# Gated cross-attention with routed experts: two of seven products added from PSUM, routing cut finer on two engines, another order of fetches, first expert block and biases

## The chip, the cores and the metric

The kernel runs on one core of one Trainium2 chip. The core has five engines with a queue of instructions each, worked off in order: TensorE (PE; its weight loads, PEld, run beside its matmuls), VectorE (DVE), ScalarE (ACT), GpSimd (POOL) and SyncE (SP, which issues DMAs here). [...]GpSimd has no part in reading PSUM here: what a matmul leaves is taken out by VectorE or ScalarE. The metric is the time of one execution on the device in microseconds, lower is better; the time of a version is the median of its runs.

## The reference

The input x is 32 sequences of 112 tokens of width 256, each with a context of 375 rows of width 256. All numbers are fp32.

```python
# cross-attention: latents = layernorm(x), context normalized too
lat = layer_norm(_layernorm(x)); ctx = layer_norm(context)
q = lat @ Wq                                   # 16 heads of 64
k, v = split(concat([ctx, lat], axis=1) @ Wkv) # 487 keys per sequence
attn = softmax(q @ k.T * 64**-0.5)
x = x + tanh(g_xattn) * ((attn @ v) @ Wout)

# experts: 8, two per token, 3584 tokens
xf = _layernorm(x)
scores = softmax(xf @ gate_w); topk_scores, topk_idx = top_k(scores, 2)
topk_scores /= sum(topk_scores)
h = gelu(xf @ w1[e] + b1[e]); y = h @ w2[e] + b2[e]
x = x + tanh(g_ffn) * sum over the two experts of (topk_score * y)
```

The expert layer is 256 to 1024 to 256 wide. A token's result needs only its two experts.

## The kernel before

**Attention loop.** The 16 heads are 8 pairs, and two sequences form a group g (16 groups). The main loop has 128 iterations n; n % 8 is the place m in the group. Each iteration attends with two head pairs of one sequence: `scores(n + 1)` (L451) makes the next iteration's scores, `nmx` (L461, VectorE) their negative maxima, `exps` (L471, ScalarE) the exponentials with their sums, `norm` (L483 `rc` on VectorE, L485 on ScalarE) divides by the sums, `turn_attn` (L492) transposes the weights four times per iteration (h = 0 to 3) into PSUM, and L496 copies each transpose to `exT` on VectorE. Every second iteration `attend` (L506) multiplies by the values, and L521 copies the result out on ScalarE.

**Sevens.** Keys and values of two sequences come from a 2x2 block product, which is done with seven products instead of eight (Strassen's way in Winograd's form): `input_sums` (L333, GpSimd, four subtractions in each group's m = 4) prepares the inputs, `seven` does the products. Each iteration does one seven's worth of products, half of a key seven and half of a value seven. Of the seven, 1, 6, 7 and 5 are copied from PSUM by ScalarE (L400, L404, L409, L414) and then added to each other on GpSimd (L394); products 2, 4 and 3 are added from PSUM by VectorE (L420). Within an iteration they stand in this order: last product and product 1, transposes h = 0; query unit (L310, L317), another last one, h = 1; product 6 and the third last one, h = 2; product 7, h = 3; product 5.

**Buffers.** All of these results, and the transposes, take their turns in the four PSUM buffers of the pool `ps_m`; the scores have two of their own. A matmul that gets a buffer waits until the instruction that empties it has run, so the place of that instruction on its engine decides when TensorE goes on.

**Order.** The order on every engine is the order in which the program is written (`tc.manual_schedule`): between the units of an iteration stand lists of filler, `pe[h]`, `dve[h]`, `soon_`, `outgoing` and `extra`, of which one part runs after each transpose h. In the filler are the layer norms of later inputs (m = 0, 2, 6, 7), the turning of inputs (m = 1, 3), and for each finished slab of 128 tokens the output projection (L541), the residual (L551), `normed` (L569, then a copy on GpSimd, L572) and the gate logits (`logits_of`, L579: eight per slab, two after each transpose, in m = 2 and 3 for one slab and m = 4 and 5 for the other).

**Routing.** Slabs are routed in groups of four (two at the end). `route_parts` gives 11 parts: largest logit, its first place, the rest, the same again for the second, then counts, places (two matmuls on PE, L665 and L668), gates and slots. One part runs after each transpose, on VectorE but for one tanh. Afterwards each token row is scattered to its place in `xg` by indirect DMAs of GpSimd (L699, eight per group, one after each transpose). The first group also finds row numbers for padded places (`strangers`, L724, L736).

**Experts.** From n = 122 (`LAST - 6`) the tail is prepared: six blocks of 128 rows are fetched (`fetch_rows`, L887, SP), then the weights of block 0 (`fetch_weights`, L900, SP). `hidden` (L918, gelu at L925 on ScalarE) and `second` (L931) do a block; blocks 0 and 1 run within n = 126 and 127. `biased` (L941) adds b2, `combine` (L947, L948) multiplies by the gate and adds the rows to the output with an indirect DMA of GpSimd. After the loop the last two slabs are projected, normalized and routed, while TensorE does blocks 0 to 2. A block's weights are fetched only if its expert isn't the one that lies there.

## Time and profile before

| | |
|---|---|
| median of 3 runs | 2190.36 us (2190.22 to 2191.26) |
| profiled execution | 2192.12 us |
| its span, first to last instruction | 2190.4 us |
| mean granted TensorE clock | 0.995 |
| scores, L451, 1024 matmuls | 242.0 us, 591 ns each |
| transposes, L492, 2048 matmuls | 283.6 us, 261 ns each |
| hidden, L918, 1920 matmuls | 229.3 us, 278 ns each |
| GpSimd additions of sevens, L394 | 1214 to 1332 ns each by form |
| DMA | 138.19 MB, mean 63 GB/s |

Busy times of engines overlap, and a matmul's duration is longer than its distance to the next, since matmuls are pipelined. A row of the timeline has start, duration, engine, line, operation, output and inputs, shapes and count; in brackets stands how long the engine had been idle before and what ended that. A row may merge several instructions that follow each other. Lines are those of the kernel before.

### The profile page before, as it was taken

What the parts mean: (1) busy time and instruction counts of PE and PEld (TensorE: products, weight loads), DVE (VectorE), ACT (ScalarE), POOL (GpSimd) and SP (SyncE); (2) the same over time, 40 slices, a digit from 0 to 9 for tenths busy, and PEclk for the clock granted to TensorE, in tenths of its full rate; (3) what the DMA queues carried; (4) which work ended last, traced back from release to release, by engine and by line L of the source; (5) the groups of instructions that cost most, each with busy time, mean ns of one, the idle gap of its engine ahead of it and who ended that gap; (6) DMA issues with size and microseconds to landing.
All of it is one profiled execution on the core that took longest, in us unless ns stands there. A gap on an engine that the chain in (4) does not pass through costs nothing. (4 is left out here: it accounts for less than half of the span.)

```text
span 2190.4 us, 41776 instructions
## 1 busy us (share of the span) xinstructions
PE 2137.0 (98%) x15944; PEld 1663.3 (76%) x15944; DVE 1251.8 (57%) x2758; ACT 1271.5 (58%) x3017; POOL 1005.3 (46%) x1136
## 2 busy tenths in 40 slices
PE   9999999999999999999999999999999899999998
PEld 5777777677777777777776777677777789999998
DVE  5567676867676767665767676756676531111111
ACT  5666666556766666667665666566665433434433
POOL 6645454455556545554546454555445222222222
PEclk9999999999999999999999999999999999999999
DMA  6692000010001000100000000000002346656553
GB/s 146 201 328 66 17 13 18 13 34 13 15 13 37 13 17 13 46 1 15 13 19 28 20 13 26 18 18 4 10 4 81 100 108 186 192 157 162 136 141 67
DMA packets 113699, 138.19 MB, mean 63 GB/s; under 512 B 14704, under 2 KB 101432, under 8 KB 113368
## 3 DMA queue, kind: packets, MB, share of 16 engines
q1 hardware_dynamic: 101032, 119.11, 17.7%
q0 software_dynamic: 11328, 15.33, 4.0%
q8 instruction: 127, 2.08, 0.4%
q10 hardware_dynamic: 1136, 1.05, 0.2%
q14 instruction: 76, 0.62, 0.1%
HBM read 166.84 MB, written 48.99 MB: 99 GB/s over the span
## 5 line engine op out<-in xcount | busy, mean ns | idle before, releaser
L485 ACT ACTIVATE ex<-ex,rc 112x487 f32<-112x487 f32 x512 | 331.1, 694 | 331.6 <-DVE rc L483 331.1
L461 DVE TENSOR_REDUCE nmx<-ps_s 112x2 f32<-112x974 f32 x256 | 287.5, 1164 | 336.8 <-PE ps_s L451 336.5
L471 ACT ACTIVATE ex<-ps_s,nmx 112x487 f32<-112x487 f32 x512 | 337.6, 668 | 152.7 <-DVE nmx L461 151.1
L496 DVE COPY exT<-ps_t 122x448 f32<-122x448 f32 x512 | 316.0, 617 | 105.7 <-PE ps_t L492 105.3
L492 PEld LDWEIGHTS ps_t<-ident,ex 112*122 112x122 f32 x2048 | 233.0, 139 | 131.4 <-issue 77.5
L925 ACT ACTIVATE h<-ps_h,b 128x128 f32<-128x128 f32 x480 | 175.5, 367 | 262.0 <-PE ps_h L918 222.0
L492 PE MATMUL ps_t<-ident,ex 112*122 112x112 f32 x2048 | 283.6, 261 | 10.1 <-ACT qT L317 3.5
L451 PE MATMUL ps_s<-kT,qT 64*112 64x487 f32 x1024 | 242.0, 591 | 0.0
L948 POOL DMA_INDIRECT out_dram<-y,xs x60 | 93.2, 1553 | 318.6 <-DVE y L947 200.1
L918 PE MATMUL ps_h<-xsT,w 128*128 128x128 f32 x1920 | 229.3, 278 | 7.5 <-issue 6.6
L918 PEld LDWEIGHTS ps_h<-xsT,w 128*128 128x128 f32 x1920 | 227.0, 194 | 12.5 <-issue 8.3
L506 PEld LDWEIGHTS ps_o<-exT,vv 122*64 122x64 f32 (+1 forms) x4096 | 197.6, 136 | 45.6 <-ACT kT L409 31.5
L931 PE MATMUL ps_y<-w,h 128*128 128x256 f32 x960 | 216.8, 379 | 0.0
L394 POOL TENSOR_TENSOR tmpv<-vv,tmpv 122x512 f32<-122x512 f32 x64 | 81.3, 1270 | 287.0 <-ACT tmpv L404 287.0
L506 PE MATMUL ps_o<-exT,vv 122*64 122x112 f32 (+1 forms) x4096 | 211.4, 260 | 0.8 <-DVE vv L420 0.8
L394 POOL TENSOR_TENSOR vv<-tmpv,vv 122x512 f32<-122x512 f32 x128 | 166.2, 1299 | 92.9 <-ACT vv L414 60.6
L384 PE MATMUL ps_v<-wkv_s,tT 128*122 128x128 f32 x1536 | 203.0, 275 | 0.2 <-POOL wkv_s L323 0.2
L378 PE MATMUL ps_k<-tT,wkv_s 128*128 128x487 f32 x378 | 191.7, 590 | 5.6 <-ACT tmpk L404 3.2
L931 PEld LDWEIGHTS ps_y<-w,h 128*128 128x128 f32 x960 | 178.0, 190 | 21.8
L384 PEld LDWEIGHTS ps_v<-wkv_s,tT 128*122 128x122 f32 x1536 | 183.1, 186 | 3.0 <-issue 1.3
L384 PEld LDWEIGHTS ps_v<-wkv,kvT 128*122 128x122 f32 x1024 | 125.8, 185 | 76.1 <-issue 53.1
L394 POOL TENSOR_TENSOR kT<-tmpk,kT 128x487 f32<-128x487 f32 x126 | 154.0, 1225 | 46.5 <-ACT kT L414 38.9
(203 smaller groups left out, 3307.1 us busy)
## 6 DMA issues: line engine op xcount, KB each, us to landing
w<-in_L_ffn_w_dram SPq DMA_DIRECT2D x120, 1024.0 KB
xg<-pad SPq DMA_DIRECT2D x8, 3640.0 KB
cin<-in_ctx_dram SPq DMA_DIRECT2D x32, 336.0 KB
xs<-xg SPq DMA_DIRECT2D x60, 130.0 KB
b<-in_L_ffn_b_dram SPq DMA_DIRECT2D x60, 128.0 KB
xin<-in_x_dram SPq DMA_DIRECT2D x32, 112.0 KB
x<-in_x_dram SPq DMA_DIRECT2D x28, 128.0 KB
out_dram<-x SPq DMA_DIRECT2D x28, 128.0 KB
```

The costliest lines, as they stand in the source:

```text
L378: nc.tensor.matmul(ps, lhsT=w[:, 0, i * P : (i + 1) * P], rhs=x[:, :NK], start=True, stop=True)
L384: nc.tensor.matmul(ps[:, c, :], lhsT=x[:, c * KC : (c + 1) * KC], rhs=w[:, 1, i * P : (i + 1) * P], start=True, stop=True,)
L394: nc.gpsimd.tensor_tensor(v[o], v[l], v[r], ALU.add)
L451: nc.tensor.matmul(ps[:, j, :NK], lhsT=qT[b // 2, i][r, b % 2, :], rhs=kT[b, i][r, :], start=True, stop=True,)
L461: nc.vector.tensor_reduce(nmx[b, i], pss[b, i][:, :, :NK], AX.X, ALU.max, negate=True)
L471: nc.scalar.activation(t[:, j, :NK], ps[:, j, :NK], AF.Exp, bias=nmx[b, i][:, j : j + 1], accum_out=sm[b, i][:, j : j + 1],)
L485: nc.scalar.mul(ex[b, i][:, j, :NK], ex[b, i][:, j, :NK], rc[:, j : j + 1])
L492: nc.tensor.transpose(ps[:, c, :], ex[b, i][:, j, c * KC : (c + 1) * KC], ident[:S, :S])
L496: nc.vector.tensor_copy(exT[b, i, j], ps)
L506: nc.tensor.matmul(ps[y * DH : (y + 1) * DH, r, x * S : (x + 1) * S], lhsT=vv[j][:m, c, x, r, y * DH : (y + 1) * DH], rhs=exT[2 * g + x, i ...
L918: nc.tensor.matmul(ps, lhsT=w1t[:, k, f * P : (f + 1) * P], rhs=xsT[t][:, k, :], start=(k == 0), stop=(k == KD - 1),)
L931: nc.tensor.matmul(psy[t], lhsT=hid[t][:, f, :], rhs=w2t[:, f, :], start=(f == 0), stop=(f == NF - 1),)
```

## The change

`exT` at h = 2 is copied by ScalarE. Products 6 and 7 are added from PSUM by VectorE. In an iteration `norm` stands directly behind the transpose's copy, ahead of the filler. Routing has 13 parts in place of 11; those that need no reduction and no PSUM go to the engine that is handed in, GpSimd in the loop and VectorE for the last group, and the first part runs two transposes earlier. The six row fetches come an iteration later, behind the weights of block 0. Block 0's first hidden unit moves from h = 0 of n = 126 to h = 1, behind both exps. `y` has three buffers of its own (two before, the pool's), and the biases of blocks 1 and 2 are added before the weight fetches that reuse their buffers.

```diff
             def p6():
                 new("t", None)
-                nc.scalar.copy(v["t"], product(6, s2, t2))
-                add("t", "11", "t")
+                nc.vector.tensor_tensor(v["t"], product(6, s2, t2), v["11"], ALU.add)
 
             def p7():
                 new("21", (a, i + NG))
-                nc.scalar.copy(v["21"], product(7, s3, t3))
-                add("21", "t", "21")
+                nc.vector.tensor_tensor(v["21"], product(7, s3, t3), v["t"], ALU.add)
...
-            nc.vector.tensor_copy(exT[b, i, j], ps)
+            (nc.scalar.copy if h == 2 else nc.vector.tensor_copy)(exT[b, i, j], ps)
...
-        def route_parts(g):
+        def route_parts(g, eng):
...
+            def equal(n, src):
+                at = new(f"s{n}", [P, RG, E])
+                nc.vector.tensor_tensor(at, src, over_e(v[f"m{n}"]), ALU.is_equal)
+                eng.tensor_tensor(at, at, over_b(rank, RG), ALU.mult)
...
             def rest():
-                first()
-                nc.vector.scalar_tensor_tensor(
-                    v["rest"], v["s1"], -BIG, logits, ALU.mult, ALU.add
-                )
+                nc.vector.tensor_tensor(v["s1"], v["s1"], over_e(v["top1"]), ALU.is_equal)
+                eng.tensor_scalar(new("rest", [P, RG, E]), v["s1"], -BIG, None, ALU.mult)
+                eng.tensor_tensor(v["rest"], v["rest"], logits, ALU.add)
 
             def apart():
-                second()
...
+                nc.vector.tensor_tensor(v["s2"], v["s2"], over_e(v["top2"]), ALU.is_equal)
...
+                eng.tensor_tensor(new("th", [P, RG]), v["m1"], v["m2"], ALU.subtract)
+                eng.tensor_tensor(new("both", [P, RG, E]), v["s1"], v["s2"], ALU.add)
+
+            def counts():
+
+                both, had = v["both"], new("had", [P, RG, E])
+                eng.tensor_copy(had[:, 0, :], macc)
+                for j in range(1, RG):
+                    eng.tensor_tensor(had[:, j, :], had[:, j - 1, :], both[:, j - 1, :], ALU.add)
+                eng.tensor_tensor(macc, had[:, RG - 1, :], both[:, RG - 1, :], ALU.add)
...
             def slots_of():
+                for s in (v["s1"], v["s2"]):
+                    eng.tensor_tensor(s, s, v["place"], ALU.mult)
...
-            ys[t] = found["tiles"].tile([P, D], F32, tag="y", name=f"y_{t}")
+            ys[t] = found["tiles"].tile([P, D], F32, tag="y", name=f"y_{t}", bufs=3)
...
-                        r, (hits, ids, ids_out) = route_parts(group[i][0])
-                        extra = [[], []] + [[part] for part in r[:10]]
+                        r, (hits, ids, ids_out) = route_parts(group[i][0], nc.gpsimd)
+                        extra = [[part] for part in r[:11]]
...
                 found["early"] = ctx.enter_context(tc.tile_pool(name="early", bufs=1, side="right"))
+                fetch_weights(0)
+            if n == LAST - 5:
                 for t in range(NE):
                     fetch_rows(t)
-                fetch_weights(0)
...
-                pe[0] += [lambda: others(ends), lambda: hidden(0, 0, 1)]
-                pe[1] += [lambda: hidden(0, 1, 3)]
+                pe[0].append(lambda: others(ends))
+                pe[1] += [lambda: hidden(0, 0, 3)]
...
                 turn_attn(n, h)
+                if more and h in (1, 3):
+                    norm(n + 1, h // 2)
                 then_ = soon_[:]
...
                     exps(n + 1, 1)
-                if more and h in (1, 3):
-                    norm(n + 1, h // 2)
...
-        r, _ = route_parts(g)
-        do(r[:7])
+        r, _ = route_parts(g, nc.vector)
+        do(r[:8])
         second(1)
+        biased(1)
         fetch_weights(4)
-        r[7]()
+        r[8]()
         second(2)
+        biased(2)
         fetch_weights(5)
```

More of the change, by code (lines that the diff above doesn't have):

```diff
@@ L594, in over_b @@
             return v.unsqueeze(1).to_broadcast([P, n, E])
-        def first_largest(src, n, g, found):
-            mx = rt.tile([P, src.shape[1]], F32, tag=f"mx{n}", name=f"mx{n}_{g}")
-            at = rt.tile([P, src.shape[1], E], F32, tag=f"sel{n}", name=f"sel{n}_{g}")
-            top = rt.tile([P, src.shape[1]], F32, tag=f"top{n}", name=f"top{n}_{g}")
-            found[f"m{n}"], found[f"s{n}"] = mx, at
-            def largest():
-                nc.vector.tensor_reduce(mx, src, AX.X, ALU.max)
-                nc.vector.tensor_tensor(at, src, over_e(mx), ALU.is_equal)
-            def where_first():
-                nc.vector.tensor_tensor(at, at, over_b(rank, src.shape[1]), ALU.mult)
-                nc.vector.tensor_reduce(top, at, AX.X, ALU.max)
-            def first():
-                nc.vector.tensor_tensor(at, at, over_e(top), ALU.is_equal)
-            return [largest, where_first, first]
-        def route_parts(g):
+        def route_parts(g, eng):
             RG, b0 = groups[g], begin[g]
@@ L626, in new, with largest @@
                 return v[tag]
-            choice = first_largest(logits, 1, g, v)
-            new("rest", [P, RG, E])
-            choice += first_largest(v["rest"], 2, g, v)
-            first, second = choice[2], choice[5]
+            def largest(n, src):
+                nc.vector.tensor_reduce(new(f"m{n}", [P, RG]), src, AX.X, ALU.max)
+            def equal(n, src):
+                at = new(f"s{n}", [P, RG, E])
+                nc.vector.tensor_tensor(at, src, over_e(v[f"m{n}"]), ALU.is_equal)
+                eng.tensor_tensor(at, at, over_b(rank, RG), ALU.mult)
@@ L633, in rest, with first @@
+            def first(n):
+                nc.vector.tensor_reduce(new(f"top{n}", [P, RG]), v[f"s{n}"], AX.X, ALU.max)
             def rest():
-                first()
-                nc.vector.scalar_tensor_tensor(
-                    v["rest"], v["s1"], -BIG, logits, ALU.mult, ALU.add
-                )
+                nc.vector.tensor_tensor(v["s1"], v["s1"], over_e(v["top1"]), ALU.is_equal)
+                eng.tensor_scalar(new("rest", [P, RG, E]), v["s1"], -BIG, None, ALU.mult)
+                eng.tensor_tensor(v["rest"], v["rest"], logits, ALU.add)
@@ L639, in apart @@
             def apart():
-                second()
-                th = new("th", [P, RG])
-                nc.vector.tensor_tensor(th, v["m1"], v["m2"], ALU.subtract)
-            choice[2], choice[5] = rest, apart
-            def both():
-                nc.scalar.activation(v["th"], v["th"], AF.Tanh, scale=0.5)
-                nc.vector.tensor_tensor(new("both", [P, RG, E]), v["s1"], v["s2"], ALU.add)
-                nc.vector.tensor_copy(new("had", [P, RG, E])[:, 0, :], macc)
-            def counts():
-                both, had = v["both"], v["had"]
-                for j in range(1, RG):
-                    nc.vector.tensor_tensor(
-                        had[:, j, :], had[:, j - 1, :], both[:, j - 1, :], ALU.add
-                    )
-                nc.vector.tensor_tensor(macc, had[:, RG - 1, :], both[:, RG - 1, :], ALU.add)
@@ L662, in places @@
-            def places():
+                nc.vector.tensor_tensor(v["s2"], v["s2"], over_e(v["top2"]), ALU.is_equal)
[7 more added lines that the diff above has]
+                eng.tensor_tensor(macc, had[:, RG - 1, :], both[:, RG - 1, :], ALU.add)
@@ L663, in places @@
+            def places():
+                nc.scalar.activation(v["th"], v["th"], AF.Tanh, scale=0.5)
                 ps = ps_m.tile([P, RG, E], F32, tag="m", name=f"ps_pos_{g}")
                 v["ps"] = ps
-                nc.tensor.matmul(
-                    ps, lhsT=before, rhs=v["both"], start=True, stop=False
-                )
+                nc.tensor.matmul(ps, lhsT=before, rhs=v["both"], start=True, stop=False)
                 nc.tensor.matmul(ps, lhsT=ones, rhs=v["had"], start=False, stop=True)
@@ L675, in gates @@
                 half = new("half", [P, RG])
-                nc.vector.tensor_scalar(half, v["th"], tg[:, 2:3], None, ALU.mult)
-                nc.vector.tensor_scalar(xr[g][:, :, 0, D], half, tg[:, 2:3], None, ALU.add)
-                nc.vector.tensor_scalar(
+                eng.tensor_scalar(half, v["th"], tg[:, 2:3], None, ALU.mult)
+                eng.tensor_scalar(xr[g][:, :, 0, D], half, tg[:, 2:3], None, ALU.add)
+                eng.tensor_scalar(
                     xr[g][:, :, 1, D], half, -1.0, tg[:, 2:3], ALU.mult, ALU.add
@@ L681, in gates, with out_to @@
                 for k in range(2):
-                    soon_.append(
-                        lambda k=k: nc.gpsimd.tensor_copy(
-                            xr[g][:, :, k, D + 1].bitcast(I32), tok[:, b0 : b0 + RG]
-                        )
+                    nc.gpsimd.tensor_copy(
+                        xr[g][:, :, k, D + 1].bitcast(I32), tok[:, b0 : b0 + RG]
                     )
             def slots_of():
-                place = v["place"]
+                for s in (v["s1"], v["s2"]):
+                    eng.tensor_tensor(s, s, v["place"], ALU.mult)
+            def out_to():
                 slot = new("slot", [P, 2, RG])
                 for k, s in enumerate((v["s1"], v["s2"])):
-                    nc.vector.tensor_tensor(s, s, place, ALU.mult)
                     nc.vector.tensor_reduce(slot[:, k, :], s, AX.X, ALU.add)
@@ L755, in strangers_out @@
                 )
-            parts = choice + [both, counts, places, gates, slots_of]
+            parts = [
+                lambda: largest(1, logits),
+                lambda: equal(1, logits),
+                lambda: first(1),
+                rest,
+                lambda: largest(2, v["rest"]),
+                lambda: equal(2, v["rest"]),
+                lambda: first(2),
+                apart,
+                counts,
+                places,
+                gates,
+                slots_of,
+                out_to,
+            ]
             return parts, (stranger_hits, stranger_ids, strangers_out)
@@ L1175 @@
                             extra.append([ids_out])
-                        extra.append(r[10:])
+                        extra += [[part] for part in r[11:]]
             if n == LAST - 8:
@@ L1258 @@
         turn_rows(3, nc.scalar.copy)
-        r, _ = route_parts(g)
-        do(r[:7])
+        r, _ = route_parts(g, nc.vector)
+        do(r[:8])
         second(1)
+        biased(1)
         fetch_weights(4)
-        r[7]()
+        r[8]()
         second(2)
+        biased(2)
         fetch_weights(5)
-        r[8]()
+        r[9]()
         found["ps"] = counted()
-        r[9]()
-        now()
-        r[10]()
+        do(r[10:])
         do(outgoing)
```

## The prediction

> **What bounds the kernel now.** I read the page's busy times first.

> ```profile
> PE 2137.0 (98%) x15944; PEld 1663.3 (76%) x15944; DVE 1251.8 (57%) x2758; ACT 1271.5 (58%) x3017; POOL 1005.3 (46%) x1136
> ```

> TensorE is busy all the time, and the change leaves its matmuls as they are. So the other engines matter only where TensorE waits for them, mostly for one of the four buffers of ps_m. To find these waits I cut the main loop into its iterations. A stretch starts at the first scores matmul (L451) emitted in iteration n and ends at the next one; the columns are its length, then busy time (and instructions) of PE, PEld, DVE, ACT and POOL, granted clock and DMA.

> ```profile
> 322.10:335.60 13.50, 13.50 (x126) 10.02 (x125) 9.00 (x22) 9.23 (x20) 10.21 (x15) 1.00 0.01 2
> 270.70:286.50 15.80, 15.17 (x133) 10.85 (x132) 11.54 (x23) 11.41 (x25) 8.68 (x8) 1.00 0.00 1
> 286.50:296.80 10.30, 10.30 (x68) 7.57 (x66) 8.12 (x19) 6.45 (x17) 4.36 (x5) 1.00 0.22 64
> 296.80:311.80 15.00, 14.49 (x127) 9.95 (x126) 10.72 (x21) 9.02 (x20) 11.41 (x10) 1.00 0.01 1
> 403.90:422.90 19.00, 16.24 (x131) 11.68 (x130) 15.19 (x35) 9.25 (x22) 10.07 (x8) 0.91 0.00 1
> 1153.80:1172.10 18.30, 15.00 (x131) 10.54 (x130) 15.38 (x34) 9.16 (x22) 10.13 (x8) 1.00 0.00 1
> 1415.40:1433.40 18.00, 15.67 (x86) 12.02 (x82) 6.50 (x11) 10.00 (x23) 15.47 (x20) 0.91 0.09 31
> 983.60:997.40 13.80, 13.80 (x86) 10.46 (x82) 6.61 (x11) 10.00 (x23) 7.99 (x13) 1.00 0.00 0
> ```

> An even iteration takes 10.3 us, an odd one 13.5 with attend (row 1), 14.34 where it also turns an input. Against these: n%8 = 3 with gate logits beside it takes 15.8 (row 2), 1.47 over 14.34, nine times; n%8 = 5 takes 14.94 (row 4; the window is rounded), 1.44 over 13.5, in 11 iterations without heavy routing. Routing makes it 19.0 and 18.2 (rows 5 and 6), and n=104 takes 18.0 where n=72 with the same work takes 13.8 (last two). The timeline of n=20 to 21 shows how the loss arises:

> ```profile
> 293.49 0.42 DVE L579 CUSTOM_DVE_ANT_0 junk<-xr,gw_sb 128x256 f32<-128x256 f32 x1
> ...
> 296.33 1.27 POOL L394 TENSOR_TENSOR tmpv<-vv,tmpv 122x512 f32<-122x512 f32 x1 [3.00 <-ACT tmpv L404]
> ...
> 296.85 1.03 DVE L579 CUSTOM_DVE_ANT_0 junk<-xr,gw_sb 128x256 f32<-128x256 f32 x1
> ...
> 297.93 1.31 DVE L579 CUSTOM_DVE_ANT_0 junk<-xr,gw_sb 128x256 f32<-128x256 f32 x1
> ...
> 299.37 1.29 ACT L485 ACTIVATE ex<-ex,rc 112x487 f32<-112x487 f32 x2 [2.62 <-DVE rc L483]
> ...
> 300.56 0.56 ACT L414 COPY vv<-ps_v 122x512 f32<-122x512 f32 x1
> ...
> 301.18 1.02 PE L310 MATMUL ps_q<-kvT,wq_sb 128*128 128x224 f32 x4 [0.19 <-ACT vv L414]
> ```

> A logit on VectorE takes 0.42 us, but 1.03 and 1.31 while a GpSimd addition runs. So rc is late, ScalarE's normalization waits 2.6 us for it, the copy of product 5 queues behind that, and the query matmuls wait for its buffer. The last view is the timeline of the end:

> ```profile
> 1718.54 1.28 ACT L925 ACT_TABLE_LOAD   x1
> 1719.84 0.37 ACT L925 ACTIVATE h<-ps_h,b 128x128 f32<-128x128 f32 x1
> 1720.22 1.28 ACT L471 ACT_TABLE_LOAD   x1
> ...
> 1722.94 1.28 ACT L925 ACT_TABLE_LOAD   x1
> ...
> 1724.65 1.00 PE L492 MATMUL ps_t<-ident,ex 112*122 112x112 f32 x4 [3.24 <-ACT h L925]
> ...
> 1779.57 0.42 DVE L941 TENSOR_TENSOR y<-ps_y,b 128x256 f32<-128x256 f32 x1 [9.80 <-DMA out_dram<-y,xs]
> ```

> The function table is loaded three times around the first expert block, and TensorE stands 3.2 us; later VectorE stands 9.8 us for a y buffer, and TensorE waits 2.0 behind it.

> **The change, part by part.** *Products 6 and 7.* Per seven, two ScalarE copies (0.54 to 0.59 us) and two GpSimd additions (1.22 to 1.33) go, and two VectorE additions with one source in PSUM come: the near row is L420, 0.66 to 0.69, which stays the same beside GpSimd work. *exT at h = 2* moves from VectorE (0.62) to ScalarE (near row: the 122x512 copies, 0.58; I take 0.55). With some 127 sevens: VectorE +254 x 0.67 - 128 x 0.62 = +91 us, ScalarE about -72, GpSimd -318. None is a time of the kernel by itself; VectorE rises to some 75% of the 1740 us loop. *norm ahead of the filler* frees ScalarE from the two logits after T3 (T0 to T3: the four transposes of an iteration).

> n%8 = 2 to 3, walked with these durations in the timeline of n=18 and 19: VectorE reaches the next maxima at 272.3 instead of 273.2, having no collisions. ScalarE still does norm, two layer norms (0.6 each) and product 5 until 274.3; two exps (1.3), the copy of product 1 (0.45), two exps, q (0.36) end at 277.8. T1 needs q's buffer and could start at 277.05. The query stall of 0.42 goes; a stall of about 0.75 at T1 stands for 0.55, and some of the 0.5 in small waits goes. I take -0.55 x 9 = -5 (ends: 0 and -13).

> n%8 = 4 to 5: here the four GpSimd subtractions of L333 (1.22 to 1.40) no longer have product 6 between them, so two run back to back from 293.3 to 296.0, on top of the first logit pair: it ends at 296.2 instead of 294.3. Product 6 is now added by VectorE behind that pair, at 296.3 to 296.9, and T3, which takes its buffer in the built program and could start at 295.46, waits until 297.0: a new stall of 1.5. Queued behind T3 are product 5 and the next scores. In return n%8 = 5 is no longer late (q, T1 and product 5 find their buffers free): -1.44. Sum 0 for 11 pairs. If the first logit gets in ahead of the subtraction, the stall is 0.6: -10 in all; the other end is +5.

> *Routing.* VectorE loses about half of its small instructions and most collisions; GpSimd gets some 15 of about 0.25 us (between L257, 125x3, 0.19, and L322, 128x128, 0.46). Where the pieces stand in n%8 = 4 GpSimd waits for VectorE's comparison between the subtractions, so the logits before it run free and T3 finds its buffer. Walking n=85: stalls of 0.4 and 1.15 plus 0.5 of position matmuls make 15.7 instead of 18.2: -2.5. n=101: -1.5. n=29 (19.0, with a stretch at clock 0.5): -3.3, and -2.5 in n=30 to 32. n=87, 88, 103 stand 1.0 to 1.1 each and n=104 4.2 because an addition for product 6 or 7 queues on GpSimd behind scatters that wait for each other, 2.7 us apart; the remaining additions of product 5 have 6 us until they are read. I count -5 for group 0, -0.5 each for 1 and 2, -4 for 3, -5.5 for 4: -15.5 (ends -8 and -20).

> *Fetches.* The six row fetches leave SP's queue one iteration later and behind the weights; they are needed at 1710, some 34 us after their issue. The last scatter of group 5 then no longer waits 6.6 us for them on GpSimd. Of 4.3 us of stalls at 1679, 1697, 1707 and 1710 I take -2.5 (0 to -4.3; the last waits for product 5's additions, which stay).

> *First expert block.* Two of three table loads go. The rows give 1.30 from load to next activation, 2.6 for two. [...]Walking ScalarE (load until 1721.0, three gelus, norm, two gelus, exT, two gelus, norm, gelu, xsT) block 1 starts at 1727.1 instead of 1731.2: -4. A stall of 2.65 remains in it. [...]The trace had the half clock after 2.65 at 408 (0.91 in its row) and not after 2.81 at 1158 (1.00): one half stretch of 3.41 would cost 1.7, leaving -2.3. I take -3.

> *Tail.* The third y buffer removes the 9.8 us wait and TensorE's 2.0. biased(2) and one more routing instruction lie on the chain to xsT of block 4; biased(1) leaves it: +0.25. SP's b2 of fetch 4 now waits for biased(1), some 3.5 us, with fetch 5 behind it and the next row fetches 14 us away, so nothing is due. Sum -1.75.

> Sum: -5 + 0 - 15.5 - 2.5 - 3 - 1.75 = -27.75. The profiled execution took 2192.1 (span 2190.4 and 1.7 around it), the median is 1.8 lower: 2192.1 - 27.75 - 1.8 = **2163**.

> **The rivals.** *The new stall at T3 doesn't come* ([...]GpSimd is later than I place it): -10 from n%8 = 4, -5 more from smaller terms: 2148. [...]against: 296.85 and 297.93, both lost. *The waits move instead of going*: the query stall becomes T1's in full, the GpSimd chain of product 5 still holds up its readers, so -5, half of routing and the -2.5 are missing: about -12.5, 2178. For it: VectorE is now the fuller engine. *Slower*: product 6's late release stalls T3 in every even iteration. In my walk the slack is 0.5 us at n%8 = 2, 0.7 at 6, over 1 at 0. Priced at 0.9 in some 49 further iterations it is +44: 2207; it decides from 28/49 = 0.57 each. *It doesn't do what it says*: evacuations weren't what TensorE waited for, 2188 to 2191; the releasers named in the rows speak against it.

> **How the numbers follow.** Forecast 0.57 (own range 2153 to 2174), T3 free 0.17, waits move 0.13, slower 0.10, no effect 0.03. The range 2144 to 2181 reaches over the first three and leaves out 0.13 and a little of their ends. Measurement tells 0.2%, 4.4 us: faster 0.87, same 0.03, slower 0.10.

> **What would show it.** Right: n%8 = 3 near 15.2 us, n%8 = 4 near 11.8 with a wait of T3 for VectorE, n%8 = 5 near 13.6, n=104 near 13.8; one gelu table load before block 0's end; no wait of y for out_dram near 1779. Wrong: T3 waiting at n%8 = 0, 2 or 6, L404 and L408 of the new code over 0.7 us, or the scatters still holding product 5's additions past their readers.

## The result

The changed kernel takes 2166.6 us (median of 4 runs, 2162.4 to 2170.8) against 2190.8 for the kernel before (2190.2 to 2194.1): ratio 0.9886, 95% interval 0.9859 to 0.9913. The forecast was 2163. The profiled execution took 2170.1 (span 2168.3), 22.1 us less of span than before; the forecast's sum was 27.75 less. Lines are now those of the changed kernel. Its busy times, to be held against those of before:

```profile
PE 2121.5 (98%) x15944; PEld 1664.4 (77%) x15944; DVE 1267.6 (58%) x2782; ACT 1203.6 (56%) x2889; POOL 711.4 (33%) x992
```

GpSimd lost 294 us and ScalarE 68; VectorE gained 16. For the products and exT alone the forecast had -318, -72 and +91; part of the routing has left VectorE for GpSimd, and of the 224 logits 65 run beside a GpSimd addition or subtraction (1013 ns each, 419 without), where 124 did before (918 ns each). None of this is time by itself. The table of windows, cut at the iterations' first scores matmul as before: n = 19, 20, 21, 29, 47, 63, 85, 104.

```profile
270.00:284.90 14.90, 14.61 (x134) 10.87 (x133) 11.22 (x25) 10.39 (x23) 3.84 (x3) 1.00 0.01 2
284.90:296.60 11.70, 10.51 (x68) 7.59 (x66) 9.54 (x19) 5.91 (x16) 6.53 (x6) 1.00 0.18 56
296.60:310.20 13.60, 13.60 (x127) 9.97 (x126) 9.94 (x23) 8.63 (x19) 3.79 (x3) 1.00 0.00 1
401.40:417.20 15.80, 14.45 (x129) 10.46 (x128) 11.82 (x31) 8.84 (x20) 7.33 (x16) 1.00 0.00 1
639.20:658.90 19.70, 17.08 (x131) 12.52 (x130) 10.51 (x26) 8.94 (x20) 9.13 (x24) 0.83 0.00 0
857.20:877.10 19.90, 17.28 (x130) 12.60 (x128) 10.56 (x26) 8.94 (x20) 9.13 (x24) 0.83 0.01 1
1152.40:1168.30 15.90, 14.54 (x131) 10.52 (x130) 11.30 (x28) 8.83 (x20) 7.84 (x18) 1.00 0.00 1
1405.10:1420.50 15.40, 14.31 (x85) 10.46 (x83) 7.17 (x12) 9.48 (x22) 8.68 (x15) 1.00 0.10 36
```

Six rows are where the forecast looked. The two at 639 and 857 are new: n=47 and 63 (groups 1 and 2, n%8=7) took 14.5 us before and take 19.7 and 19.9, at clock 0.83. The timeline of n=20, the forecast's new stall:

```profile
292.84 1.41 POOL L333 TENSOR_TENSOR tT<-kvT,tT 128x488 f32<-128x488 f32 x1
...
293.21 1.32 DVE L577 CUSTOM_DVE_ANT_0 junk<-xr,gw_sb 128x256 f32<-128x256 f32 x1
...
294.46 0.68 DVE L404 TENSOR_TENSOR tmpv<-ps_v,vv 122x512 f32<-122x512 f32 x1
...
295.20 0.60 PE L490 MATMUL ps_t<-ident,ex 112*122 112x112 f32 x4 [1.19 <-DVE tmpv L404]
```

The logit takes 1.32 beside the subtraction, product 6's addition comes after it, and T3 waits 1.2 for that addition. The timeline of n=47 shows what the forecast had not seen:

```profile
642.84 1.27 POOL L394 TENSOR_TENSOR vv<-vv 122x512 f32<-122x512 f32 x1
...
644.40 0.89 POOL L249 TENSOR_TENSOR rsc<-vec,nhalf 125x3 f32<-125x3 f32 x1
...
646.94 0.19 POOL L257 TENSOR_TENSOR sh<-vec,rsc 112x1 f32<-112x1 f32 x1
647.07 0.19 POOL L632 COPY had<-macc 128x8 f32<-128x8 f32 x1
647.34 0.76 POOL L634 TENSOR_TENSOR had<-had,both 128x8 f32<-128x8 f32 x3
...
648.15 0.64 PE L642 MATMUL ps_pos<-had,ones 128*128 128x32 f32 x2 [2.62 <-POOL had L634]
```

`counts` now runs on GpSimd. There it stands behind product 5's additions and then behind the roots of the next inputs' layer norms (L248 to L257, 644.1 to 647.1), which stand in n%8=7 up to n=111. TensorE, whose second position matmul needs `had`, stands 2.6 us, and two stretches of 3.41 us at half clock follow; stall and clock together make up the 5.2 and 5.4. In the kernel before, the same iteration had the counts on VectorE, and that matmul did not wait:

```profile
655.12 0.54 DVE L657 TENSOR_TENSOR had<-had,both 128x8 f32<-128x8 f32 x3
...
655.79 0.39 PE L668 MATMUL ps_pos<-had,ones 128*128 128x32 f32 x2
```

### The profile page after: what moved, and what is told of

Read it like the earlier page. It is cut to its first block, busy times and chain, and to the rows that moved or that the text cites. A ratio compares the mean times of both kernels' runs of the same rounds, so it can differ in the third digit from the quotient of the medians.

```text
span 2168.3 us, 41569 instructions
## 1 busy us (share of the span) xinstructions
PE 2121.5 (98%) x15944; PEld 1664.4 (77%) x15944; DVE 1267.6 (58%) x2782; ACT 1203.6 (56%) x2889; POOL 711.4 (33%) x992
## 5 line engine op out<-in xcount | busy, mean ns | idle before, releaser
L483 ACT ACTIVATE ex<-ex,rc 112x487 f32<-112x487 f32 x512 | 331.0, 694 | 360.8 <-DVE rc L481 358.9
L490 PE MATMUL ps_t<-ident,ex 112*122 112x112 f32 x2048 | 283.8, 261 | 17.3 <-DVE tmpv L404 13.1
L494 DVE COPY exT<-ps_t 122x448 f32<-122x448 f32 x384 | 236.9, 617 | 38.4 <-PE ps_t L490 38.4
L394 POOL TENSOR_TENSOR vv<-tmpv,vv 122x512 f32<-122x512 f32 x64 | 81.3, 1270 | 467.4 <-ACT vv L412 447.3
L394 POOL TENSOR_TENSOR kT<-tmpk,kT 128x487 f32<-128x487 f32 x63 | 77.0, 1222 | 305.4 <-ACT kT L412 305.2
L418 DVE TENSOR_TENSOR kT<-ps_k,kT 128x487 f32<-128x487 f32 x189 | 124.5, 659 | 50.3 <-PE ps_k L378 43.7
```

The lines of the kernel that those rows point to most:

```text
L483: nc.scalar.mul(ex[b, i][:, j, :NK], ex[b, i][:, j, :NK], rc[:, j : j + 1])
L490: nc.tensor.transpose(ps[:, c, :], ex[b, i][:, j, c * KC : (c + 1) * KC], ident[:S, :S])
L494: (nc.scalar.copy if h == 2 else nc.vector.tensor_copy)(exT[b, i, j], ps)
```

## The experiments

The table holds what the verdicts rest on: lengths of iterations in each profile (us, from one first scores matmul to the next), the stretch from the loop's last scores to the last attend, span and median. "products" is the kernel before with part of the change; the others are the changed kernel with one or two things different.

| | before | products alone | old routing | routing on VectorE | changed | counts ahead | logits behind 6 | both |
|---|---|---|---|---|---|---|---|---|
| n=19 (like 6 of n%8=3) | 15.81 | 14.86 | 14.88 | 14.86 | 14.86 | 14.88 | 14.86 | 14.86 |
| n=20 (like 11 of n%8=4) | 10.31 | 12.00 | 11.72 | 11.71 | 11.72 | 11.72 | 10.31 | 10.31 |
| n=21 (like 11 of n%8=5) | 14.96 | 13.60 | 13.55 | 13.55 | 13.55 | 13.55 | 14.20 | 14.20 |
| n=28 (84 alike; 100 too, but 10.83 before) | 10.48 | 12.32 | 12.05 | 12.04 | 10.31 | 10.31 | 10.31 | 10.31 |
| n=29 | 18.98 | 15.44 | 14.89 | 14.97 | 15.87 | 15.87 | 16.01 | 16.01 |
| n=47 | 14.53 | 14.70 | 14.50 | 14.07 | 19.70 | 13.94 | 19.76 | 13.95 |
| n=63 | 14.53 | 14.70 | 14.49 | 14.06 | 19.90 | 13.94 | 18.42 | 13.94 |
| n=88 | 18.17 | 18.04 | 18.10 | 17.22 | 17.22 | 17.22 | 17.22 | 17.22 |
| n=104 | 17.98 | 15.99 | 16.02 | 15.75 | 15.42 | 15.23 | 15.60 | 15.81 |
| last scores to last attend | 22.37 | 22.34 | 18.46 | 18.47 | 21.06 | 20.99 | 21.08 | 18.47 |
| span, profiled | 2190.4 | 2174.1 | 2159.8 | 2158.5 | 2168.3 | 2157.8 | 2160.3 | 2149.3 |
| median | 2190.8 | 2176.9 | 2161.3 | 2160.4 | 2166.6 | 2158.7 | 2157.0 | 2149.4 |

The kernel before had medians of 2193 to 2195 beside the experiments, so ratios to it are given where whole times are compared.

**Counts ahead of the roots.** In the loop's filler the counts go ahead of the list with the roots; both stay on GpSimd.

```diff
+            counts.ahead = True
...
+                ahead_ = bool(extra) and hasattr((extra[0] + [None])[0], "ahead")
+                if ahead_:
+                    do(extra.pop(0))
                 then_ = soon_[:]
...
-                if extra:
+                if extra and not ahead_:
                     do(extra.pop(0))
```

> The changed kernel with one difference: on GpSimd the counts of a group (L632 to L635) run ahead of the layer norms' roots (L248 to L257), not behind them. In the changed kernel's profile n=47 and n=63 take 19.7 and 19.9 us (14.5 before): TensorE stands 2.6 us at the second position matmul (L642) for had, which lies behind 3.0 us of roots and these behind product 5's additions, and two stretches of 3.41 us at half clock follow. Theory of the place in the queue: both fall to about 14.5, -10.5 in all on the profiled execution (2170.1 to about 2159.6), and the runs lose the difference between 2162 and 2171, which would be the half clock that follows the stall or not. Rival, GpSimd is too slow for the counts wherever they stand: they end 1.2 us after product 5's additions, so about 1 us of stall stays and the iterations take 15.5 to 17. Rival, the roots are now late for the inputs' scaling: the loss moves to n=48 and n=64, about 1 us each. Rival, the half clock comes for another reason: the mean clock stays at 0.994 or 0.995 in some runs.

Measured: n=47 and 63 13.94, span -10.5, 2158.7 us (2157.2 to 2159.5, 5 runs; ratio 0.9835, 0.9821 to 0.9848). The spread of the runs falls from 8.4 us to 2.3, the clock of four of them is 0.997 to 0.999. The timeline of n=47 in this version:

```profile
642.60 1.27 POOL L394 TENSOR_TENSOR vv<-vv 122x512 f32<-122x512 f32 x1
643.81 0.19 POOL L632 COPY had<-macc 128x8 f32<-128x8 f32 x1
644.08 0.76 POOL L634 TENSOR_TENSOR had<-had,both 128x8 f32<-128x8 f32 x3
644.89 0.30 PEld L641 LDWEIGHTS ps_pos<-both,before 128*128 128x128 f32 x2
...
645.13 0.39 PE L642 MATMUL ps_pos<-had,ones 128*128 128x32 f32 x2
```

`had` is ready when TensorE gets there. The place in the queue was the cause, not GpSimd's pace, and nothing came later at n=48 (17.22 in both). The two iterations gave 11.7 us; in this profile a half-clock stretch fell on n=85 (17.55 for 15.87), which took 1.7 of it back.

**Logits behind products 6 and 3.** Only the first logit pair of n%8=4 moves, on VectorE alone.

```diff
-                        dve[h].append(lambda h=h, i=i: logits_of(i, 2 * h - 2, 2 * h))
+                        (pe[2] if (u, h) == (1, 1) else dve[h]).append(
+                            lambda h=h, i=i: logits_of(i, 2 * h - 2, 2 * h)
+                        )
```

> The changed kernel with the first pair of gate logits of n%8=4 written behind products 6 and 3 instead of ahead of them; same work otherwise. In the changed kernel n%8=4 takes 11.72 us in 11 iterations, since product 6's addition (L404) waits behind two logits that GpSimd's subtractions lengthen to 1.23 and 1.32, and T3 waits for its buffer. Theory: the order on VectorE is the cause. T3's buffer is free at about 292.6 instead of 295.1, n%8=4 falls to about 10.4; at n%8=5 the query unit then comes 1.4 earlier and waits some 0.6 for product 5's copy, so the net is -0.8 in each of 11: about -9 (ends -5 and -15). Rival, VectorE is the bound over the two iterations together: n%8=5 grows by what n%8=4 loses, net 0. Half-clock stretches behind n=47 and 63 stay and add up to 8 us of spread, so the iterations of the profile decide, not the medians.

Measured: n%8=4 10.31 and n%8=5 14.20 (+0.65), -8.3 over the 11 pairs; 2157.0 us (ratio 0.9829, 0.9814 to 0.9844). Its timeline of n=20:

```profile
292.20 0.69 DVE L404 TENSOR_TENSOR tmpv<-ps_v,vv 122x512 f32<-122x512 f32 x1
...
293.02 1.23 POOL L333 TENSOR_TENSOR tT<-kvT,tT 128x488 f32<-128x488 f32 x1
293.53 1.00 DVE L577 CUSTOM_DVE_ANT_0 junk<-xr,gw_sb 128x256 f32<-128x256 f32 x1
294.02 0.55 PE L490 MATMUL ps_t<-ident,ex 112*122 112x112 f32 x4
```

The addition starts 2.3 us earlier, T3 waits no more, and the logit that still meets a subtraction (1.00) has nobody behind it whom TensorE needs at once. Half of the 1.41 comes back at n%8=5, as expected.

**Routing of before, everything else changed.** `route_parts` and its schedule are those of the kernel before.

> The changed kernel with the routing of before: 11 parts on VectorE, starting two transposes later, everything else changed. Theory of the forecast: n=29 to 32, 85, 100 and 101 gained by the routing's new cut (-3.1, -1.0, -1.3, -0.5, -2.35, -0.5, -1.3 in the profile, -10 in all) and turn back; n=47 and 63 go back to 14.5 (-10.5); n=87, 88, 103, 104 gained by products 6 and 7 leaving GpSimd (-5.7 in all) and stay. Net about 0 against the changed kernel's profile: 2170, and 2165 to 2168 if the half clock falls otherwise. Rival: the gains at n=29, 85 and 101 too come from the missing collisions with GpSimd's additions; then they stay, and the routing of before gives about 2159, better than the change as a whole.

Measured: 2161.3 us (2160.5 to 2163.0; ratio 0.9850, 0.9835 to 0.9865). The rival won: n=29, 85 and 101 don't go back to 19.0, 18.2 and 17.2 but fall below the changed kernel, to 14.9. Their gain is that of the missing collisions: with the same routing the four logits of n=29 took 0.76, 1.31, 0.41 and 1.37 us before and take 0.40, 0.42, 0.60 and 0.42 here. The new cut costs these iterations 1.0 each. It pays at n=28, 84 and 100 (12.05 to 10.31), since there GpSimd waits for VectorE between the subtractions, so that two logits are done by then, and 0.9 at n=88. The changed kernel's timeline of n=28:

```profile
398.89 0.19 DVE L610 TENSOR_TENSOR s<-rest,m 128x32 f32<-128x32 f32 x1
...
399.16 0.25 POOL L611 TENSOR_TENSOR s<-s,rank 128x32 f32<-128x32 f32 x1 [1.30 <-DVE s L610]
```

Over the loop the routing's new cut brings -3.3 us, and +10.6 at n=47 and 63.

**Products alone.** The kernel before with products 6 and 7 on VectorE and the third transpose on ScalarE.

```diff
-                nc.scalar.copy(v["t"], product(6, s2, t2))
-                add("t", "11", "t")
+                nc.vector.tensor_tensor(v["t"], product(6, s2, t2), v["11"], ALU.add)
...
-            nc.vector.tensor_copy(exT[b, i, j], ps)
+            (nc.scalar.copy if h == 2 else nc.vector.tensor_copy)(exT[b, i, j], ps)
```

> The kernel before with products 6 and 7 added from PSUM by VectorE and the third transpose copied by ScalarE; the softmax division stays behind the filler, routing, fetches, first block and tail as before. Theory of the forecast, the collisions made rc late: n%8=4 11.7 (+1.4 in 11), n%8=5 13.6 (-1.4 in 11), n%8=3 about 15.3 (-0.5 in 9), n=87, 88, 103, 104 -5.7 together, some 2 of n=29 to 32: about -12, 2178. Rival, it is the place of the division that matters: n%8=5 stays at 14.9 and n%8=3 at 15.8, so only the stalls at T3 (+15) and the -5.7 are left: about 2200, slower than before. Rival, neither: T3's wait doesn't come while the division stands behind the filler: 2170.

Measured: 2176.9 us (2175.9 to 2181.2; ratio 0.9927, 0.9911 to 0.9942), span -16.3. n%8=5 falls to 13.6 and n%8=3 to 14.86 with `norm` still behind the filler: the collisions made `rc` late, not its place. The two logits ahead of `rc` at n=21 take 0.41 and 0.43 us where they took 1.03 and 1.31. What `exT`'s move alone is worth was not separated. What `norm`'s move is worth shows against the column "old routing": 12.00 to 11.72 at T3, 15.44 to 14.89 at n=29, about -6.9 from the loop's start to its last scores; the fetches, which differ too, have at most 0.3 of it (below).

**Both edits.** Counts ahead and logits behind 6.

> The changed kernel with both earlier edits: counts ahead of the roots on GpSimd, and the first logit pair of n%8=4 behind products 6 and 3. If the two losses are independent, as their places say, they add: -10.5 of n=47 and 63 and -0.76 in each of 11 pairs (n%8=4 10.3, n%8=5 14.2), -8.3: from the changed kernel's profiled execution of 2170.1 to 2151, runs within 3 us of each other. Rival: the stall at n%8=5 grows where the iteration before it is shorter, or the half clock now falls on other places: 2155 or more.

Measured: 2149.4 us (2149.0 to 2152.4; ratio 0.9801, 0.9788 to 0.9815). The two losses were independent and add. In its profile one half-clock stretch fell on n=85 (17.67 for 16.0), and none on the first expert block, where the changed kernel has two. This is 17 us below the changed kernel by the medians, and beats both kernels. The group of transposes, whose waits for L404 were 13.1 us in the changed kernel, has none left:

```profile
L490 PE MATMUL ps_t<-ident,ex 112*122 112x112 f32 x2048 | 281.5, 259 | 4.6 <-ACT qT L317 2.9 <-DVE kT L418 1.5 <-DVE exT L494 0.2
```

**Three routings with the logits right.** First the routing of before with the later logits, then the thirteen pieces with `nc.vector` in place of `nc.gpsimd`, without and with the later logits.

> The changed kernel with the routing of before (11 parts on VectorE) and the first logit pair of n%8=4 behind products 6 and 3. Theory: with the routing on VectorE n=28, 84 and 100 have the T3 stall as well (12.05 for 10.31), so the later logits win in all 14 even iterations: -0.76 in 11 and about -1.2 in 3 against the run with the routing of before (2161): 2149, as good as or better than both edits on the new routing, which would say that the new cut of the routing brought nothing. Rival: VectorE, which has the whole routing, is now too full at n=29, 85 and 101: they rise from 14.9 to over 17, and this version ends at 2153 or more.

> The changed kernel with the thirteen routing pieces of the loop all on VectorE, so that the engine is told apart from the cut. Theory: n=47 and 63 lost on GpSimd's queue and return to 14 to 14.5 (-10.5); n=28, 84 and 100 lose what they gained, since GpSimd no longer waits for VectorE between the subtractions (10.3 to 12.05, +5.2), n=29, 85 and 101 go from 15.9 to about 15 (-2.7): -8 in all, about 2161. Rival: the pieces cost VectorE more than the collisions did: n=29, 85 and 101 rise towards the 17 to 19 of before, and the run ends at 2168 or more.

> The changed kernel with the thirteen pieces all on VectorE and the first logit pair of n%8=4 behind products 6 and 3. From the two runs that had one of the edits each: n%8=4 10.3 in all 14, n%8=5 14.2 in 11 and 15.6 in the three with routing, n=47 and 63 14.1, the rest as with the routing on VectorE: 2160.4 - 0.76 x 11 - (1.7 - 0.6) x 3 = 2148.7, within 1 us of the version with both edits: GpSimd's share in the routing is worth nothing once the order of the logits is right. Rival: GpSimd's share matters: 2152 or more.

Measured: 2153.0 (2149.3 to 2154.4), 2160.4 (2159.5 to 2161.9) and 2151.3 us (2150.6 to 2155.3). Taking the pieces off GpSimd brings n=47 and 63 to 14.1. With the later logits all three routings lie within 4 us: the first has n=28 at 10.33 and n=29 at 15.60, the third 11.51 and 15.69, since two pieces of the routing (L610, L611) now stand ahead of product 6 on VectorE and take 0.99 and 1.15 us beside the subtractions, so that T3 waits 0.76 (part of the rival's case), and "both" 10.31 and 16.01. The first and the third miss their forecasts, 2149 and 2148.7. In the profiles the loop's last scores start at 1680.0 in the first, 1683.2 in the third and 1682.0 in "both"; the first expert block, where these two have half-clock stretches and "both" none, is then 2.6 and 2.5 us longer. Which engine routes matters little; what stands in front of what matters.

**First expert block as before.** `hidden(0, 0, 1)` ahead of the first transpose of n=126 again.

> The changed kernel with the first expert block's parts placed as before (one hidden part ahead of the first transpose of n=126, so two more loads of the function table). Theory: two loads of 1.28 us stand in ScalarE's way again; block 1 starts about 16.4 us after the last scores of the loop instead of 13.4, and the part from those scores to the end, 469.5 in the changed kernel's profile, grows by 1.3 to 3, according to where the half clock falls (the changed kernel has two stretches of it there, 1705.5 and 1712.4). Rival: the loads were hidden and the start moved with something else: less than 0.5.

Measured: block 1 starts 16.20 us after the loop's last scores (13.43 in the changed kernel, 16.38 before), the last attend 22.19 after them (21.06), and the part from those scores to the end 470.8 (469.5). 2170.9 us (2168.2 to 2171.2). The two loads of 1.28 stood in the way.

**Biases, and fetches, as before**, on the version with both edits.

> The version with both edits (2149.4) with the tail's biases as before: two y buffers and no biases of blocks 1 and 2 ahead of the routing. Measured from the last attend to the first hidden matmul of the eighth block of the sequence, 39.3 us in the version with both edits and 43.7 in the kernel before. Theory of the forecast: VectorE waits again some 10 us for a y buffer, TensorE 2 behind it, the chain to the fifth xsT is 0.7 longer: +2.6 without half clock, up to +4.4 with one stretch of it. Rival, what helped was something else in the tail: less than +0.5.

> The version with both edits (2149.4) with the six row fetches one iteration earlier and ahead of the first weights, as before. Forecast of this term: +2.5 at n=121 to 125. Theory now: the kernel with products alone has the old fetches and loses at n=121, 123 and 124 only 0.25, 0.36 and 0.06 against the one with the routing of before, so +0.7 at most, inside the spread of the runs: the iterations decide. Rival, the forecast's size holds: n=121 to 125 together 2 us longer.

Biases: 2155.7 us (2154.7 to 2157.0; ratio 0.9830, 0.9815 to 0.9845), +6.3. Blocks are numbered from 0 here; the mark that the expectation calls the eighth block is block 5, and it comes 43.1 us after the last attend. Timeline of the tail, an addition of b2 and block 5's matmuls:

```profile
1742.76 0.42 DVE L930 TENSOR_TENSOR y<-ps_y,b 128x256 f32<-128x256 f32 x1 [9.89 <-DMA out_dram<-y,xs]
...
1744.01 5.44 PE L907 MATMUL ps_h<-xsT,w 128*128 128x128 f32 x32 [3.55 <-issue]
```

The wait for a y buffer is back. It holds up the copy of block 5's xsT and TensorE by 3.55, and the block runs at half clock (5.44 for 3.81). Blocks 3 to 5 take 7.08, 11.04 and 8.95 us instead of 6.61, 7.32 and 7.32: +5.8, of which the half clock is about 1.6. In that profile the first expert block also met two half-clock stretches, which "both" has not (+2.6), so the +6.3 is not all of the buffer's making. Fetches: 2149.7 us (2148.8 to 2151.8) for 2149.4; n=121 to 125 take 65.27 for 65.00. Nothing measurable.

**Scatters behind two transposes only**, on the version with both edits.

```diff
-                if outgoing:
+                if outgoing and (h < 2 or n > 112):
```

> The version with both edits, with the routed rows' scatters written behind the first two transposes of an iteration only, not behind all four (from n=113 on as before). Forecast's step for n=104: product 5's additions queue on GpSimd behind scatters that wait for each other, 2.7 us apart; that is the 1.6 to 2.0 us that n=104 still has over the 13.8 of n=72. Theory: two scatters fewer stand ahead of the additions, which then start when their copy is done: n=104 13.8 to 14.2, about -1.7, 2147.7 to 2148, and n=87, 88 and 103 unchanged. Rival: the wait at n=104 is for something else and stays at 15.2 to 15.8; then no gain.

Measured: n=104 13.77 for 15.81, as long as n=72 with the same work. GpSimd before this edit:

```profile
1395.10 0.96 POOL L673 DMA_INDIRECT xg<-xr,sloti  x1 [1.82 <-DVE exT L494]
1396.09 1.23 POOL L394 TENSOR_TENSOR kT<-tmpk,kT 128x487 f32<-128x487 f32 x1
```

and with it:

```profile
1386.16 0.96 POOL L673 DMA_INDIRECT xg<-xr,sloti  x1 [1.83 <-DVE stc L227]
1387.59 1.22 POOL L394 TENSOR_TENSOR kT<-tmpk,kT 128x487 f32<-128x487 f32 x1 [0.47 <-ACT kT L412]
```

The addition no longer stands behind the scatters, it waits for its own copy. The median does not show the 2 us (2149.8, 2149.0 to 2150.9). The edit costs 1.25 at n=37 (15.45 for 14.21): the scatters of group 0 now reach into n=36 and delay a subtraction there, so that two subtractions lie beside one logit:

```profile
509.13 2.24 DVE L577 CUSTOM_DVE_ANT_0 junk<-xr,gw_sb 128x256 f32<-128x256 f32 x1
```

Besides, half-clock stretches fell on the first expert block and on the tail of this profile, which are 0.9 and 1.3 us longer than in "both", where one fell on n=85.

## Why the prediction held, point by point

| step | forecast | in the profile |
|---|---|---|
| n%8=2 to 3 (nine) | -5 | -7.9 |
| n%8=4 to 5 (eleven pairs) | 0 | +0.3 |
| routing, n=28 to 32, 84 to 88, 100 to 104 | -14.5 | -16.0 |
| routing, groups 1 and 2 | -1 | +10.5 |
| fetches, n=118 to 125 | -2.5 | -2.2 |
| first expert block, to the last attend | -3 | -1.3 |
| tail behind the last attend | -1.75 | -4.8 |
| the rest (n=0 and small) | 0 | -0.7 |
| sum | -27.75 | -22.1 |

**The new stall at T3** came as worked out: +1.41 against the forecast 1.5, L404 and L408 at 0.63 to 0.69, and -1.39 at n%8=5 against -1.44. The first logit pair took 1.23 and 1.32 us beside the subtractions in all eleven iterations (0.42 without), so the rival of 2148 fell (what lies behind these collisions no run here shows), and the slower rival had no footing: n%8 = 0, 2 and 6 show no new wait of T3.

**n%8=3** went to 14.86, not 15.2. The mechanism was right, the size was off: VectorE reaches the next maxima at 271.55, not at 272.3 as walked, and T1 waits 0.29 for q's copy instead of 0.75. And "norm ahead of the filler frees ScalarE" had no part in it, since products alone reach 14.86. Of the 0.5 left over 14.34 that wait is 0.3; the rest was not looked into.

**Routing** is the step that failed. The forecast priced GpSimd's pieces one by one ("some 15 of about 0.25 us") and walked groups 0, 3 and 4. Groups 1 and 2 got "-0.5 each" without a walk. They start at n%8=5, so their counts fall on n%8=7, where the roots are queued. The step lacked the question that the forecast asked elsewhere: what stands ahead of `had` on its new engine, and who waits for it. Answer: 3.0 us of roots, and TensorE; 2 x 2.6 us, and a stretch of 6.83 us at half clock behind each. The credit was also placed wrongly: most of what groups 0, 3 and 4 gained came with products 6 and 7 and `exT` ("products alone": 18.98 to 15.44 at n=29), not from the routing's cut.

**n=104** takes 15.42, not 13.8. It kept 1.65 of its stall, because not only the additions of products 6 and 7 but those of product 5 queue behind the scatters; the last experiment shows it. The forecast had said that these "have 6 us until they are read", and had named the opposite among its signs of being wrong; that sign came true here.

**Fetches** had the right sum for a wrong reason: undone alone they cost 0.3 us, and products alone, with the old fetches, have 1.7 of the 2.2 already (1.2 of it at n=123, 16.34 to 15.10).

**First expert block**: block 1 starts 2.95 earlier, within 0.05 of the forecast, but this agreement is luck: the 3 was set between the walk's 4 and the 2.3 with one half-clock stretch. Two such stretches fell here (at 1705.52, behind a step of the last section's grid with 1.65 us of idle, and at 1712.35, behind one with 1.99), and the second one cost 1.6 behind block 1. Where none fell ("both", old routing) last scores to last attend takes 18.47, -3.9, which is the -4 of the walk; the kernel before has half clock of its own in this part (6.8 us from 1722.8), so this is not the loads' worth alone. The reading that the half-clock term rested on was wrong: the stalls near 408 and 1158 in the kernel before are equally long,

```profile
410.68 1.02 PE L310 MATMUL ps_q<-kvT,wq_sb 128*128 128x224 f32 x4 [2.65 <-ACT vv L414]
...
1160.64 1.02 PE L310 MATMUL ps_q<-kvT,wq_sb 128*128 128x224 f32 x4 [2.65 <-ACT vv L414]
```

and they differ in how the grid of the last section cuts them: 2.02 of the first lies in one step, of the second only 1.59. That this sets them apart is my reading of the counts given there. The price of the load was the row's: 1.28 us at each of the three loads of the kernel before in this part and at the one of the changed kernel, with 0.02 of idle before it and 0.01 behind it. The load and the stall in the changed kernel:

```profile
1703.83 1.28 ACT L913 ACT_TABLE_LOAD   x1
...
1712.21 1.93 PE L906 MATMUL ps_h<-xsT,w 128*128 128x128 f32 x8 [1.99 <-POOL macc L635]
```

(ScalarE and TensorE; the copy of xsT by ScalarE, which ended at 1712.1, came last, not the releaser named.)

**Tail**: mis-sized. The forecast counted TensorE's 2.0 and +0.25 for the chain. The chain got 0.66 shorter: TensorE's wait for the xsT of block 4 went from 3.24 to 2.58 (first line before, second line changed; 32 matmuls take 5.44 with half clock, 3.81 without).

```profile
1769.87 5.44 PE L918 MATMUL ps_h<-xsT,w 128*128 128x128 f32 x32 [3.24 <-issue]
...
1751.52 3.81 PE L906 MATMUL ps_h<-xsT,w 128*128 128x128 f32 x32 [2.58 <-issue]
```

The half clock behind this wait went with it, 1.6, and the forecast had no term for that. Another 0.4 was gained ahead of block 3. The wait for a y buffer has moved to 1797.8 (5.5 us), where TensorE does not wait for it.

That the total was near is luck: the 11.5 lost against the forecast in groups 1 and 2 was partly made up by 2.9 at n%8=3, 3.0 in the tail and 1.5 in the other groups, none of them foreseen in this size. The median, too, lies between two pairs of runs. These runs, two near 2162.7 at clock 0.998 and two near 2170.4 at 0.994 and 0.995, differ by 7.7 us, by my estimate what the clock accounts for: 0.0035 of 2165 us is 7.6.

## What to carry to other kernels

When work moves to another engine, walk its queue at every place where it occurs, not at the heaviest: the same small piece was free in four groups and cost 5 us in two. When VectorE and GpSimd share a load, an instruction that TensorE waits for belongs ahead of the ones that took longer beside GpSimd (a logit 1.01 us on average for 0.42); moving the logits was worth 8.3 us, the choice of engine after it at most 4. And look at the granted clock behind TensorE's longest stalls: at n=47 the 2.6 us of stall and the 6.83 us at half clock behind it cost 5.8 us together (19.70 against 13.94 with the counts ahead), so these stalls are the first to remove.

## What the runs showed of the hardware

| time without a matmul in a step | steps | next step at half clock |
|---|---|---|
| 1.99 to 2.71 us | 6 | 6 |
| 1.52 to 1.85 us | 7 | 2 (1.65 and 1.85) |
| 1.21 us or less | 1230 | 0 |

Two stalls of the changed kernel, nearly equally long, were cut differently: of the 2.62 us up to 648.15, 1.85 lay in the step that ends at 647.39, and half clock began there; the 2.58 at 1749 was cut into 0.96 and 1.62, and full clock went on. What grants the clock no run here shows. Nor is it shown that such stretches made the spread between runs, 8.4 us in the changed kernel and 2.3 with the counts ahead: the runs without a profile show their mean clock, not where their stretches lie.

**VectorE beside GpSimd.** In the changed kernel a logit took 0.42 us without a GpSimd addition (L394) or subtraction (L333) of 1.2 us or more beside it (159 times) and 1.01 on average with one (65 times, 0.42 to 1.38), while VectorE's addition of 122x512 with one source in PSUM (L418) took 0.68 beside one (48 times) and 0.69 otherwise (144 times). The operation alone does not decide it: in the kernel before, L606 (128x32), a TENSOR_TENSOR too but with both sources in SBUF, took 1.20 beside one (3 times) and 0.19 otherwise (9 times).
